# One block of 105 empty TensorE instructions, or 140 spread in fives: a cross-attention layer on one core

## The chip, the core and the metric

The kernel runs on one core of a Trainium2 chip. The metric is device time in microseconds (us), less is better. TensorE is called PE here (its weight loads PEld), VectorE DVE, ScalarE ACT, GpSimd POOL and SyncE SP. SP issues nearly all DMAs.

## The reference

128 sequences of 128 tokens, 256 features, 16 heads of 16 features, all in float32. `x` gives the queries, a second sequence `c` gives keys and values. What is computed, cut to its core:

```
q, k, v = heads(x @ Wq + bq), heads(c @ Wk + bk), heads(c @ Wv + bv)
scores  = q @ k.T / 4, and -1e30 wherever j >= i        # a strictly lower triangle
attn    = softmax(scores); the row i = 0 is set to 0
x1      = layer_norm(x + (attn @ v) @ Wo + bo, ln1)
out     = layer_norm(x1 + relu(x1 @ W1 + b1) @ W2 + b2, ln2)
```

The hidden layer has 1024 features.

## The kernel before

The batch is worked in 64 pairs of sequences. Each pair passes through several steps of a software pipeline, since its stages lie far apart: step p does the scores, the softmax and the values of pair p, the weighted sum and the output projection of pair p-2, the first hidden product of pair p-3, the second one of pair p-4, the second norm of pair p-6, and queries and keys of pair p+1.

Nothing is scheduled by a compiler. The order on every engine is the order in which the code is written. There are three stretches of it:

- **The front**: steps 0 to 8, written out; from step 7 on as a long list of `do("name", p)` calls, one operation a line. It ends with `do("h4", 7)` and `do("v4", 8)` (L2410 and L2411).
- **The steady part**: `for p in range(9, 61): step(p)`, 52 steps. `step` (L1761) walks the string `ORDER` (from L1746), in which every operation has its place; a suffix such as `-1` means that it belongs to the step before.
- **The tail**: steps 61 to 63, written out again.

What a step asks of PE, in the order of `ORDER`: `weigh` (L586 and L596: probabilities times values, 96 small matmuls in the trace, read from `brought`), `scores` (L440: 64 small matmuls, queries `qT` times keys `kT`), and then 30 products of five families. `v1` to `v4`, `o1` to `o4`, `q1` to `q4` and `k1` to `k4` (L1147, values, output, queries, keys) have 1 to 3 matmuls of 128x128 each, `w1` to `w7` (L1147, second hidden product) and `h1` to `h7` (L1358, first hidden product) 4 each. Each float32 matmul of the program appears as two MATMULs and two LDWEIGHTS in the trace.

Results of PE lie in eight banks of PSUM. `scores` writes all eight, so it needs what the other engines still read there to be done: the copies of the value product (`vr`, ACT L1272), `hf` (DVE L1383), and the rectified hidden layer (`re0` on DVE L1397, `re1` to `re3` on ACT L1399). `ro0` to `ro3` (ACT L1387) follow; they read no bank. `context` (DVE L612 and L617) takes the result of `weigh`. `h4` writes to a bank that `ha` (DVE L1377) has to have read.

SP's DMAs within a step, in order: `br0` to `br3` (L552: the transposed probabilities, `brought<-turned`, 128 KB each), the loads of a coming pair (L92: `xb` in one step, `cb` in the next, four of 128 KB each), in every second step a load of 512 KB of raw tokens (L99, `x<-in_x_dram`), the store of a finished pair (L765, 256 KB), and `ks2` and `ks` (L1235, `kT<-kr`, 128 KB each), which `scores` of the next step waits for.

`empty(n)` (L251) puts n instructions on PE that do nothing (NO_OP in the built program, NOP in the trace, L253). Two tables place them: `EMPTY` puts 2 to 5 behind each of the 30 products of a step of the steady part, 101 in all; `LEAD` puts n ahead of a whole step, and holds one entry, 105 ahead of step 9. The front's own products of steps 7 and 8 have none.

Counted in the built program, a step of the steady part has 768 PE instructions: 328 MATMULs, 328 LDWEIGHTS, 101 NOPs and 11 waits that stand by themselves. The whole PE program before has 48,035.

Of the kernel before, what the change touches and what calls it, by code (L numbers as in the profile page):

```python
# [19 lines left out]
def tile_cross_attention_block(  # L20
# [230 lines left out]
    def empty(n):  # L251
        for _ in range(n):
            nc.tensor.nop(hint="pad", nofuse=True)  # L253
# [1502 lines left out]
    """.split()  # L1756

    EMPTY = {'w1': 5, 'h1': 4, 'w2': 5, 'h2': 4, 'w3': 5, 'h3': 5, 'w4': 4, 'h4': 5, 'w5': 4, 'h5': 5, 'w6': 4, 'h6': 5, 'w7': 5, 'h7': 4, 'v1': 3, 'o1': 2, 'q1': 2, 'k1': 2, 'v2': 3, 'o2': 2, 'q2': 2, 'k2': 3, 'v3': 2, 'o3': 2, 'q3': 3, 'k3': 2, 'v4': 2, 'o4': 2, 'q4': 3, 'k4': 2}
    LEAD = {9: 105}

    def step(p):  # L1761

        empty(LEAD.get(p, 0))
        for key in ORDER:
            key, late = (key.split("-") + ["0"])[:2]
            q = p - int(late)
            if FIRST <= q < NP - 1:
                OPS[key](q)
                if key in EMPTY:
                    empty(EMPTY[key])  # L1770
# [76 lines left out]
    def do(key, p):  # L1847
        OPS[key](p)
# [443 lines left out]
    do("res1", 7)  # L2292
    do("eh6", 8)
    do("q1", 8)
    do("o1", 8)
    do("w1", 7)
    do("eh7", 8)
    do("w5", 7)
    do("add1", 8)
    do("lowmax", 8)  # L2300
    do("v3", 8)
    do("el0", 8)
    do("w2", 7)
    do("add2", 8)
    do("tokc", 7)
    do("qk", 8)
# [3 lines left out]
    do("xc1", 7)  # L2310
    do("max2", 8)
    do("o2", 8)
    do("wk", 7)
    do("finish1", 7)
    do("ok2", 8)
# [1 line left out]
    do("max1", 8)  # L2317
    do("el7", 8)
    do("k1", 8)
    do("xc3", 7)  # L2320
    do("cc1", 8)
    do("cc3", 8)
    do("add0", 8)
    do("vb", 8)
    do("w3", 7)
    do("q2", 8)
    do("max0", 8)
    do("el3", 8)
    do("o3", 8)
    do("tokx", 8)  # L2330
    do("w6", 7)
    do("load", 7)
    do("kk", 8)
    do("br3", 8)
# [4 lines left out]
    do("oa", 8)  # L2339
    do("xs0", 7)  # L2340
    do("k2", 8)
    do("qk2", 8)
    do("xs2", 7)
    do("o4", 8)
    do("q3", 8)
    do("xs1", 7)
    do("el5", 8)
    do("eh2", 8)
# [5 lines left out]
    do("res1", 8)  # L2354
    do("stats2", 8)
    do("w7", 7)
    do("or", 8)
    do("kk2", 8)
    do("h1", 7)
    do("va", 8)  # L2360
    do("qb", 8)
    do("eh4", 8)
# [3 lines left out]
    do("eh5", 8)  # L2366
    do("el4", 8)
    do("h2", 7)
    do("wb", 7)
    do("wa", 7)  # L2370
    do("stats1", 8)
    do("means", 8)
    do("el1", 8)
    do("k3", 8)
    do("w4", 7)
    do("deviations", 8)
    do("h6", 7)
    do("hk2", 7)
    do("qa", 8)
    do("hb", 7)  # L2380
# [2 lines left out]
    do("el2", 8)  # L2383
    do("kb", 8)
    do("h5", 7)
    do("hk5", 7)
    do("xc0", 8)
    do("ka", 8)
    do("wr", 7)
    do("k4", 8)  # L2390
    do("xc1", 8)
    do("store", 7)
    do("h7", 7)
    do("turn0", 8)
    do("turn1", 8)
    do("kr", 8)
    do("recip", 8)
    do("ks2", 8)
    do("q4", 8)
    do("ha", 7)  # L2400
    do("h3", 7)
    do("qr", 8)
    do("norm2", 8)
    do("turn2", 8)
# [3 lines left out]
    do("addbo", 8)  # L2408
    do("ks", 8)
    do("h4", 7)  # L2410
    do("v4", 8)  # L2411
    for p in range(9, 61):
        step(p)

# [650 lines left out]
```

## Time and profile before

| what | value |
|---|---|
| time, median of 3 runs (lowest, highest) | 1499.5 us (1498.47, 1502.43) |
| the profiled execution: its own time | 1498.78 us |
| the profiled execution: span, first to last instruction | 1497.0 us |
| mean granted TensorE clock over the span | 0.993 |
| DVE, ACT, POOL busy | 1374.0, 1304.2, 1265.4 us |
| one step in the middle, 239.66 to 261.68 us: PE, DVE, ACT, POOL busy | 21.85, 21.30, 20.88, 19.58 of 22.02 us |
| DMA: bytes moved, mean rate | 220.33 MB, 147 GB/s |

The times of the profile are counted from the span's start. "Busy" is the time in which an engine had an instruction in work. Sequencer work (NOPs, waits, DMA issues) does not count as busy. "Idle before" is the pause of an engine ahead of an instruction with what seems to have ended it; "issue" there means that nothing in the profile was waited for. Pauses below 0.15 us are not listed as such.

### The profile page before, as it was taken

Reading aid. Unit: us, or ns where it says so; the run is one execution under the profiler, and the core shown is the slowest. Engines: PE = TensorE matmul, PEld = TensorE weight load, DVE = VectorE, ACT = ScalarE, POOL = GpSimd, SP = SyncE. Lnnn points to the kernel's source line nnn. Section 1 sums busy time; section 2 is a strip of 40 time slices with the busy share of each in tenths; the row PEclk is TensorE's granted clock in tenths of the full one; section 3 lists DMA queues with packets and bytes.
Section 4 is the critical chain, followed back from the end, with each engine's and each line's share of the span. In section 5 each row is a group of like instructions: output and inputs, shape, how many; then the busy total and the mean of one; then the engine's idle time right before and its main releaser. Section 6 shows DMA issues by size and latency. Waiting matters only on the chain.

```text
span 1497.0 us, 61901 instructions
## 1 busy us (share of the span) xinstructions
PE 1458.7 (97%) x20713; PEld 1399.8 (94%) x20713; DVE 1374.0 (92%) x3231; ACT 1304.2 (87%) x5559; POOL 1265.4 (85%) x1816
## 2 busy tenths in 40 slices
PE   9999789999999999999999999999999999999998
PEld 7788789999999999999999999999999999999988
DVE  7987879999999999999999999999999999998767
ACT  5668879999989999999999999989999999998743
POOL 6967768888988988988988988988988988888966
PEclk9999999999999999999999999999999999999999
DMA  8274657666766766766766766766766766764541
GB/s 200 72 152 105 162 125 160 149 159 150 169 146 156 158 151 150 165 155 154 156 151 152 170 146 150 156 155 150 170 152 153 167 149 150 164 153 119 123 112 50
DMA packets 367448, 220.33 MB, mean 147 GB/s; under 512 B 279600, under 2 KB 335152, under 8 KB 367152
## 3 DMA queue, kind: packets, MB, share of 16 engines
q1 hardware_dynamic: 364864, 214.27, 63.1%
q8 instruction: 187, 3.06, 0.9%
q10 hardware_dynamic: 2288, 2.11, 0.6%
q14 instruction: 109, 0.89, 0.2%
HBM read 55.06 MB, written 18.09 MB: 49 GB/s over the span
## 4 chain that ended last, share of the span: by engine, by line
PE 75%; ACT 8%; DVE 6%; DMA 4%; SPq 3%; POOL 2%; issue 2%; DVEq 0%; ACTq 0%; POOLq 0%
PE banks L1147 38%; PE banks L1358 19%; ACT sm L931 6%; PE banks L440 5%; PE banks L596 3%; DMA kT<-kr 3%; SPq L552 2%; PE banks L869 2%; PE banks L586 2%; PE banks L300 1%; DMA brought<-turned 1%; PE banks L971 1%; PE banks L629 1%; DVE sm L464 1%; ACT kr L1213 1%
## 5 line engine op out<-in xcount | busy, mean ns | idle before, releaser
L931 ACT ACTIVATE sm<-banks,nmx 128x128 f32<-128x128 f32 x944 | 336.8, 383 | 16.4 <-DVE nmx L1558 12.8
L931 ACT ACTIVATE sm<-sm,nmx 128x64 f32<-128x64 f32 x944 | 321.6, 368 | 1.4 <-DVE nmx L920 1.4
L533 DVE STREAM_TRANSPOSE turned<-sm 128x1024 f32<-128x1024 f32 x186 | 217.1, 1214 | 4.7 <-DMA brought<-turned 2.9
L931 ACT ACTIVATION_READ_ACCUMULATOR sm<-banks,nmx 128x1 f32 x944 | 211.2, 224 | 0.0
L931 ACT ACTIVATION_READ_ACCUMULATOR sm<-sm,nmx 128x1 f32 x944 | 206.9, 219 | 0.0
L1147 PE MATMUL banks<-wt,hS 128*128 128x128 f32 x1344 | 177.5, 275 | 0.0
L1358 PE MATMUL banks<-xS,w1t 128*128 128x128 f32 x1344 | 177.2, 275 | 0.0
L1147 PEld LDWEIGHTS banks<-wt,hS 128*128 128x128 f32 x1344 | 163.6, 192 | 0.0
L1358 PEld LDWEIGHTS banks<-xS,w1t 128*128 128x128 f32 x1344 | 163.4, 192 | 0.0
L1558 DVE TENSOR_REDUCE nmx<-banks 128x4 f32<-128x512 f32 x224 | 152.3, 680 | 1.9
L1547 POOL TENSOR_TENSOR hS<-hT 128x512 f32<-128x512 f32 x116 | 147.7, 1274 | 5.0 <-ACT hT L876 2.4
L1358 PE MATMUL banks<-brought,w 128*128 128x128 f32 x896 | 118.2, 275 | 0.0
L1534 POOL TENSOR_TENSOR oc<-cxT 128x128 f32<-128x128 f32 x112 | 48.9, 457 | 80.4 <-DVE cxT L617 76.9
L1608 POOL TENSOR_TENSOR x1b<-x,g_r 128x512 f32<-128x512 f32 x56 | 72.3, 1290 | 52.3 <-ACT x L703 52.3
L1147 PE MATMUL banks<-w,hT 128*128 128x128 f32 x896 | 109.8, 275 | 0.0
L1358 PEld LDWEIGHTS banks<-brought,w 128*128 128x128 f32 x896 | 109.0, 192 | 0.0
L440 PE MATMUL banks<-kT,qT 32*64 32x128 f32 (+1 forms) x3840 | 101.2, 333 | 4.7 <-DMA kT<-kr 3.3
L1147 PEld LDWEIGHTS banks<-w,hT 128*128 128x128 f32 x896 | 104.8, 192 | 0.1
L440 PEld LDWEIGHTS banks<-kT,qT 32*64 32x64 f32 x3840 | 83.0, 132 | 15.5 <-issue 5.0
L1387 ACT ACTIVATE hT<-hT,b1e_c 128x256 f32<-128x256 f32 x224 | 95.7, 509 | 1.2 <-DVE hT L1383 1.1
L596 PE MATMUL banks<-brought,vz 128*32 128x64 f32 x4096 | 88.2, 223 | 6.6 <-issue 6.6
L1552 DVE TENSOR_TENSOR banks<-banks,neg 128x256 f32<-128x256 f32 x224 | 93.2, 417 | 0.0
(322 smaller groups left out, 4836.2 us busy)
## 6 DMA issues: line engine op xcount, KB each, us to landing
brought<-turned SPq DMA_DIRECT2D x936, 128.0 KB, 2.4
out_dram<-t SPq DMA_DIRECT2D x63, 256.0 KB, 4.6
xb<-in_x_dram SPq DMA_DIRECT2D x124, 128.0 KB, 3.1
cb<-in_ctx_dram SPq DMA_DIRECT2D x124, 128.0 KB, 3.2
x<-in_x_dram SPq DMA_DIRECT2D x31, 512.0 KB, 5.0
kT<-kr SPq DMA_DIRECT2D x112, 128.0 KB, 2.9
brought<-turned SPq DMA_DIRECT2D x40, 96.0 KB, 2.5
w<-in_L_xattn_W_dram SPq DMA_DIRECT2D x2, 1024.0 KB, 7.9
```

The costliest lines, as they stand in the source:

```text
L440: nc.tensor.matmul(st["sps", hi][r][s * HP : (s + 1) * HP, m * 2 * n : (m + 1) * 2 * n].rearrange("p (e j) -> p e j", e=2), st["qT"][strip ...
L533: nc.vector.transpose(turned[:, :, at : at + 256].rearrange("p j (n a) -> p n j a", a=32), states[p]["sm", hi].rearrange("p h j -> p (h j) ...
L596: nc.tensor.matmul(pc[32 * j : 32 * j + 32, at + HP : at + P], st["vz"][:, s, 4 * m + j, 2 * e : 2 * e + 2, :].rearrange("p e d -> p (e d) ...
L931: nc.scalar.activation(sm[:, h, :], src, AF.Exp, bias=nmx[:, h : h + 1], scale=1.0, **({"accum_out": st["su"][:, at : at + 1]} if summed e ...
L1147: nc.tensor.matmul(out, left(k) if self.depth > 1 else left, right(k) if self.depth > 1 else right, start=(n == 1 and k == 0), stop=(k == ...
L1358: nc.tensor.matmul(ps[:, i * P : (i + 1) * P].rearrange("p (n a) -> p n a", a=32), left(i), right, start=(n in (1, 2, 5) and i == 0), stop ...
L1387: nc.scalar.activation(self.hT[:, f, at], self.hT[:, f, at] if src is None else src, AF.Relu, bias=b1e_c[:, f : f + 1], scale=1.0,)
L1534: nc.gpsimd.tensor_tensor(c[:, n], left, right, how)
L1547: engine.tensor_tensor(c[:, n], left, right, how)
L1552: nc.vector.tensor_tensor(ps[:, :, HP:], ps[:, :, HP:], neg[:, 1, None, :].to_broadcast([P, 4, HP]), ALU.add)
L1558: nc.vector.tensor_reduce(states[p]["nmx", 1][:, 4 * b : 4 * b + 4], banks[:, b].rearrange("p (n j) -> p n j", j=P), AX.X, ALU.max, negate ...
L1608: nc.gpsimd.tensor_tensor(st["x1b"], st["x1b"] if n else st["x1"], (be1b_r if n else g1_r)[:, None, :].to_broadcast([P, 2, D]), ALU.add if ...
```

## The change

`LEAD` becomes empty, and 28 calls of `empty(5)` are put into the front, each behind one of the last 28 PE products that the front has for steps 7 and 8, from `q1` of step 8 to its last, `v4`. The diff, cut:

```diff
-    LEAD = {9: 105}
+    LEAD = {}
...
     do("q1", 8)
+    empty(5)
     do("o1", 8)
+    empty(5)
     do("w1", 7)
+    empty(5)
     do("eh7", 8)
     do("w5", 7)
+    empty(5)
...
     do("o4", 8)
+    empty(5)
     do("q3", 8)
+    empty(5)
...
     do("q4", 8)
+    empty(5)
     do("ha", 7)
     do("h3", 7)
+    empty(5)
...
     do("h4", 7)
+    empty(5)
     do("v4", 8)
+    empty(5)
     for p in range(9, 61):
         step(p)
```

Only PE's list of instructions changes; on DVE, ACT, POOL and SP the same operations stand in the same order. The built PE list at the end of the front (`q4`, `h3`, `h4` and `v4`, then the first matmuls of `weigh` of step 9), before:

```order
L1147 MATMUL banks<-xT_2247,wqt 128x128
L1358 MATMUL banks<-xS_2623,w_132 128x128 x4
L1358 MATMUL banks<-brought,w1t 128x128 x4
L1147 MATMUL banks<-wvt,cT_2245 128x128
L253 NO_OP x105
L586 MATMUL banks<-brought,vd_180 32x64 x8
```

The same place in the changed program:

```order
L1147 MATMUL banks<-xT_2247,wqt 128x128
L253 NO_OP x5
L1358 MATMUL banks<-xS_2683,w_132 128x128 x4
L253 NO_OP x5
L1358 MATMUL banks<-brought,w1t 128x128 x4
L253 NO_OP x5
L1147 MATMUL banks<-wvt,cT_2245 128x128
L253 NO_OP x5
L586 MATMUL banks<-brought,vd_180 32x64 x8
```

Five of the 105 are left between `v4` and `weigh`; the others are gone from this place. The middle of the front, where short products follow each other (`o3`, `w6`, `k2` and `o4`; `cc`, `oc` and `hS` are sums that POOL made), before and after as one difference:

```order
 L1147 MATMUL banks<-wot,oc_2443 128x128
+L253 NO_OP x5
 L1147 MATMUL banks<-wt,hS_2269 128x128 x4
-L1147 MATMUL banks<-cc_2563,wkt 128x128
-L1147 MATMUL banks<-cc_2563,wk 128x128
-L1147 MATMUL banks<-wot,cxT 128x128
+L253 NO_OP x5
+L1147 MATMUL banks<-cc_2593,wkt 128x128
+L1147 MATMUL banks<-cc_2593,wk 128x128
+L253 NO_OP x5
+L1147 MATMUL banks<-wot,cxT 128x128
+L253 NO_OP x5
```

Behind each product, five NOPs are new; the products themselves stand as they did (the numbers behind the names are buffers). All of the steady part and of the tail keeps its instructions, but stands 35 instructions further back in the PE program, which has 48,070.

More of the change, by code (lines that the diff above doesn't have):

```diff
@@ L2329, in tile_cross_attention_block @@
     do("o3", 8)
+    empty(5)
     do("tokx", 8)
     do("w6", 7)
+    empty(5)
     do("load", 7)
@@ L2341, in tile_cross_attention_block @@
     do("k2", 8)
+    empty(5)
     do("qk2", 8)
@@ L2344, in tile_cross_attention_block @@
     do("o4", 8)
+    empty(5)
     do("q3", 8)
+    empty(5)
     do("xs1", 7)
@@ L2356, in tile_cross_attention_block @@
     do("w7", 7)
+    empty(5)
     do("or", 8)
@@ L2359, in tile_cross_attention_block @@
     do("h1", 7)
+    empty(5)
     do("va", 8)
@@ L2368, in tile_cross_attention_block @@
     do("h2", 7)
+    empty(5)
     do("wb", 7)
@@ L2374, in tile_cross_attention_block @@
     do("k3", 8)
+    empty(5)
     do("w4", 7)
+    empty(5)
     do("deviations", 8)
     do("h6", 7)
+    empty(5)
     do("hk2", 7)
@@ L2385, in tile_cross_attention_block @@
     do("h5", 7)
+    empty(5)
     do("hk5", 7)
@@ L2390, in tile_cross_attention_block @@
     do("k4", 8)
+    empty(5)
     do("xc1", 8)
@@ L2393, in tile_cross_attention_block @@
     do("h7", 7)
+    empty(5)
     do("turn0", 8)
@@ L2399, in tile_cross_attention_block @@
     do("q4", 8)
+    empty(5)
     do("ha", 7)
     do("h3", 7)
+    empty(5)
     do("qr", 8)
@@ L2410, in tile_cross_attention_block @@
     do("h4", 7)
+    empty(5)
     do("v4", 8)
+    empty(5)
     for p in range(9, 61):
```

## The prediction

> **What bounds the kernel now.** I read the page first, then the waits of PE between 200 and 1400 us, then timelines.
>
> ```profile
> span 1497.0 us, 61901 instructions
> PE 1458.7 (97%) x20713; PEld 1399.8 (94%) x20713; DVE 1374.0 (92%) x3231; ACT 1304.2 (87%) x5559; POOL 1265.4 (85%) x1816
> q8 instruction: 187, 3.06, 0.9%
> PE banks L596 <- issue: 6.6, 14, 1.1
> PE banks L440 <- DMA kT<-kr: 3.3, 9, 0.7
> ```
>
> PE is busy 97% of the span. In the 1200 us of the steady part it waits (columns: us in total, times, longest) in two places only: 14 times inside `weigh` for "issue", which is nothing that the profile shows, and 9 times ahead of `scores` for the `kT` DMA. PE is the bound there, so a pause that leaves PE shortens the run by as much, unless another wait steps in. The timeline of PE where the front ends, and the windows beside it (busy us and count of PE, PEld, DVE, ACT, POOL; granted clock; DMA share and GB/s):
>
> ```profile
> 183.47 1.16 PE L1358 MATMUL banks<-brought,w1t 128*128 128x128 f32 x8 [0.90 <-DVE hT L1377]
> 184.46 0.39 PE L1147 MATMUL banks<-wvt,cT 128*128 128x128 f32 x2
> 191.87 0.66 PE L586 MATMUL banks<-brought,vd 128*32 128x64 f32 x16 [7.02 <-issue]
> 194.59 2.16 PE L440 MATMUL banks<-kT,qT 32*64 32x128 f32 x64
> ...
> 186.00:188.00 2.00, 0.00 (x0) 0.00 (x0) 0.73 (x2) 2.00 (x7) 0.06 (x1) 1.00 0.00 0
> 188.00:190.00 2.00, 0.00 (x0) 0.00 (x0) 0.00 (x0) 0.39 (x1) 0.00 (x0) 0.75 0.00 0
> 190.00:192.00 2.00, 0.13 (x8) 0.16 (x11) 0.00 (x0) 0.00 (x0) 0.00 (x0) 0.50 0.00 0
> 192.00:194.00 2.00, 2.00 (x81) 2.00 (x84) 0.00 (x0) 0.00 (x0) 0.00 (x0) 0.50 0.03 8
> 194.00:196.00 2.00, 2.00 (x67) 1.73 (x64) 0.89 (x4) 0.00 (x0) 0.39 (x1) 0.55 0.00 0
> ...
> L253 PEldq NOP  x93: 13/13/13, 184.5 to 191.4; - x93
> ```
>
> PE stands still for 7.02 us between `v4` (184.46) and `weigh` of step 9 (191.87). The last row, the NOPs between 184.5 and 192.5 us, says what it does: 93 of the 105 start there in 6.9 us, one every 75 ns (the 13 in the row is what the record calls their length). The other 12 ran while `h4` and `v4` were still at work. Behind the pause the granted clock is 0.50 until about 195 us, so `weigh` and `scores` run at half speed. From 189 to 194 us no engine does anything. This is one place where the whole chip waits for empty instructions.
>
> **The change, first part: the 105 go.** What `weigh` and `scores` cost at full clock is in any later step without a stall, such as step 11:
>
> ```profile
> 238.18 0.43 PE L586 MATMUL banks<-brought,vd 128*32 128x64 f32 x16
> 239.66 1.67 PE L440 MATMUL banks<-kT,qT 32*64 32x128 f32 x64
> ...
> 185.61 1.20 ACT L1399 ACTIVATE hT<-banks,b1e_c 128x256 f32<-128x256 f32 x3 [0.46 <-DVE hT L1397]
> 186.69 1.70 ACT L1387 ACTIVATE hT<-hT,b1e_c 128x256 f32<-128x256 f32 x4
> 197.66 0.27 ACT L1686 COPY vz<-banks 128x128 f32<-128x128 f32 x1 [9.26 <-PE banks L1147]
> 186.04 0.69 DVE L1614 STREAM_TRANSPOSE turned<-x 128x512 f32<-128x512 f32 x1
> 181.56 1.36 SPq L1235 DMA_DIRECT2D kT<-kr  x2
> kT<-kr SPq DMA_DIRECT2D x112, 128.0 KB, 2.9
> ```
>
> From the start of `weigh` to the end of `scores` step 11 takes 1.48 + 1.67 = 3.15 us; step 9 takes 191.87 to 196.75, 4.88. So the half clock costs 1.73 us.
>
> Without the block, `weigh` can start when `v4` is done, at 184.85, or 0.1 us later: `v4`'s own five NOPs (0.37 us) and four single waits come after it in the sequencer, which ran ahead of `v4`. Then `scores` starts at 184.95 + 1.48 = 186.4 and ends at 188.1. What it needs is there in time: `re1` to `re3` end at 186.81 and are needed in the second half of `scores`; `kT`'s two DMAs are issued by 182.92 and land 2.9 us after their issue, by 185.9; DVE is free for `context` from 186.73. Behind `scores`, ACT's first work for step 9 (197.66 before) moves to about 189.0, and `ro0` to `ro3` are done at 188.39. POOL and SP have nothing left from before. In step 10 the same ACT work ends about as long behind `weigh` as here, so nothing is compressed beyond what a normal step does.
>
> The term: 7.02 − 0.10 + 1.73 = **8.65 us less**. It is bounded above by 8.8 (no gap at all) and below by about 7: if `scores` had to wait for the end of ACT's `ro` (188.39) instead of starting at 186.4, 2.0 us would come back.
>
> **Second part: 140 NOPs behind the front's products.** At 75 ns five take 0.37 us of PE's sequencer. They cost nothing as long as the array still has queued work:
>
> ```profile
> 172.58 0.39 PE L1147 MATMUL banks<-wot,oc 128*128 128x128 f32 x2
> 172.80 1.06 PE L1147 MATMUL banks<-wt,hS 128*128 128x128 f32 x8
> 173.70 0.39 PE L1147 MATMUL banks<-cc,wkt 128*128 128x128 f32 x2
> ```
>
> A product of one program matmul occupies the array 0.22 us (172.58 to 172.80), one of four 0.90. Eight of the 28 have one matmul, so they fall short by 0.15 us each, 1.2 us in all if no lead is left; the long ones win 0.5 us each. The cover is the sequencer's lead. If it is gone everywhere, PE reaches `h4` up to 1.2 us late, and there it has 0.90 us to spare, since it waits for DVE until 183.47 anyway. I take 0 and bound it by 0 and 0.3 us.
>
> **Third part: everything behind stands 35 instructions later.** The q8 row counts 187 fetches of 3.06 MB, 16.4 KB each; the PE program has 48,035 instructions, so a fetch brings 257, or the round 256. A step has 768, three times that. So the borders between fetched blocks fall at the same three places in every step. One lies in `weigh`:
>
> ```profile
> 260.21 0.43 PE L586 MATMUL banks<-brought,vd 128*32 128x64 f32 x16
> 261.12 0.39 PE L596 MATMUL banks<-brought,vz 128*32 128x64 f32 x10
> 262.06 0.54 PE L596 MATMUL banks<-brought,vz 128*32 128x64 f32 x22 [0.55 <-issue]
> 262.52 0.69 PE L440 MATMUL banks<-kT,qT 32*64 32x128 f32 x24
> ...
> 217.17 0.54 PE L596 MATMUL banks<-brought,vz 128*32 128x64 f32 x22 [0.23 <-issue]
> 217.64 1.66 PE L440 MATMUL banks<-kT,qT 32*64 32x128 f32 x64
> 1378.20 1.10 PE L440 MATMUL banks<-kT,qT 32*64 32x128 f32 x29
> ...
> 239.66:261.68 22.02, 21.85 (x312) 21.34 (x306) 21.30 (x53) 20.88 (x93) 19.58 (x29) 1.00 0.74 169
> ```
>
> In steps 12 and 10, PE stops behind the tenth matmul of the last group, with 22 left: behind matmul 74 of 96, both times. All 14 stalls stand on L596. From `scores` of step 10 (217.64) to `scores` of step 62 (1378.20) are 52 steps in 1160.56 us; at 22.02 us for a step without a loss (the window in the last row, from `scores` of step 11 to the stall of step 12) they would take 1145.04. So **15.5 us** are lost at `weigh` and `scores`, more than the listed 6.6 + 3.3, since pauses below 0.15 us are not listed. All of it can be touched by a shift of the border.
>
> When is a block asked for? The place 256 instructions ahead of the stalling one has 26 NOPs between it and `weigh`; the place 35 further ahead has 31. Two answers on L253 (windows 209.6 and 209.0 to 215.6), two on DMA queues (214.8 to 216 and 231 to 234 us), and SP's timeline:
>
> ```profile
> L253 PEldq NOP  x26: 13/13/13, 209.6 to 214.5; - x26
> L253 PEldq NOP  x31: 13/13/13, 209.0 to 214.5; - x31
> q8 instruction: 1, 0.02, 4.9%
> q8 instruction: 1, 0.02, 3.3%
> 209.77 0.62 SPq L99 DMA_DIRECT2D x<-in_x_dram  x1
> ```
>
> In the products of step 9 the sequencer passes that place at about 209.5 us, and the fetch runs only between 214.8 and 216, some 5 us later (the stall at 217.17); in those of step 10, which has no 512 KB load, it runs before 234 and nothing stalls (238.18 above). In step 9 SP issues that load at 209.77, just behind the request. So the stall is a fetch that came out late from behind a big load, in every second step.
>
> In the changed kernel the border lies 35 instructions earlier in the step, still in `weigh`, behind matmul 56 or 57. PE gets there 17.5 x 15.4 ns = 0.27 us earlier (96 matmuls in 1.48 us), and the request goes out 0.6 us earlier by the NOPs. **Bounds**: if late fetches come out at the same time as before, because the load ahead of them sets it, each of 14 stalls grows by 0.27, 3.8 us more. If the 0.6 us pass through, each shrinks by 0.33, 4.6 us less. If the request gets ahead of the load in all steps, nearly the whole loss goes, 12 of 15.5 us, the rest staying with `kT`. The nearest row is the 0.6 us between request and load: 209.0 instead of 209.6, load at 209.77. I take **3 us less**, since part of each stall hides a wait for `kT` that takes its place.
>
> Runtime: NRT & Kernel Launch of the Trainium skill, section Instruction fetch mechanics, says that blocks of 256 instructions are fetched while the one before executes, and that crossing a border is mostly hidden. By it this term would be 0; the trace agrees with the size of the block (257 by count) and not with the hiding (6.6 us on L596).
>
> **The sum**: 8.65 + 0 + 3 = 11.7 us less. The profiled execution has a span of 1497.0 and took 1498.8 us, 1.8 around it; 1498.8 − 11.7 = 1487.1. The median of the runs is 0.7 above that execution: 1499.5 − 11.7 = **1488 us**. About 0.3%, 4.5 us, is what a measurement of this kernel tells from no change.
>
> **Rivals.**
>
> *The border in the new place costs nothing.* The request precedes the load in every second step, fetches come early, `kT`'s engine is not held up: 8.65 + 12 = 20.6 less, **1479 us**. For it: steps without the load never stall. Against: 0.6 us is a small head start, and the load's four smaller predecessors are already under way.
>
> *The new place is neutral or worse in the same steps.* Late fetches stay where they are, and stalls grow by 0.27 us: 8.65 − 3.8 = 4.9 less, **1494.6 us**; with the skill's hidden fetch or with gains and losses that cancel, 8.65 less, 1490.9.
>
> *Slower.* Also the steps without the load begin to stall at the border. Price: each of 52 steps 0.17 us makes up for the 8.65; with 0.55, the stall of step 12, in the 26 steps that have none, and 3.8 in the others, 14.3 + 3.8 − 8.65 = 9.5 more, **1509 us**. It decides from the point where the fetch of such a step starts later than about 2.4 us ahead of PE's arrival. Against: there the fetch ended before 234, over 4 us ahead of 238.18, and PE arrives only 0.27 us earlier.
>
> *The change doesn't hide the NOPs.* If every NOP of the 140 took its 75 ns from PE, 10.5 us would come back, 1498.5 us with the 3. Against: PE's lead and the 0.90 us in front of `h4`.
>
> **How the numbers follow.** Forecast (the lead gone, the border worth between −1 and +7 us): 0.50, 1483 to 1492, likeliest 1488. Border free: 0.20, 1478 to 1483. Border worse: 0.20, 1492 to 1496. Slower: 0.05. NOPs not hidden: 0.05. The range 1479 to 1496 leaves out the upper two and a little of the second. Faster by over 0.3% (below 1495.0): 0.50 + 0.20 + 0.15 = 0.85. Within: 0.05 of the border worse, 0.05 of the NOPs: 0.10. Slower: 0.05.
>
> **What would show it.** `weigh` of step 9 within 0.3 us behind the front's `v4`, clock 1.00 in all windows from 180 to 200 us, `scores` of step 9 near 186.4: first part. `h4` of the front still at 183.5, with a shorter wait on DVE L1377: second part. Stalls on L586 behind 56 or 57 matmuls instead of L596 behind 74, their sum against 6.6, and the 52 steps from `scores` to `scores` against 1160.6 us: third part. The prediction is wrong if those 52 steps take over 1165 or under 1152 us, or if the stretch before step 10 gains less than 7.

## The result and the profile after

The changed kernel takes 1478.36 us (median; 1476.86 to 1482.84) against 1498.99 us before: ratio **0.9864, 95% interval 0.9837 to 0.9891**. That is 20.6 us less where 11.7 were forecast, 0.6 us below the range. Beside later runs of the kernel before it gave 1480.4 (0.9876, 0.9855 to 0.9896) and 1482.0 us (0.9869, 0.9844 to 0.9893), so 18 to 20 us less. The profiled execution took 1482.84 us, the longest of the four. One profile, that of the 140 in a block below, fell into a disturbed state at a clock of 0.848, so that only the times of that kernel are used.

The head of the page, and PE's waits between 175 and 1400 us, after:

```profile
span 1481.1 us, 61936 instructions
PE 1454.3 (98%) x20713; PEld 1398.6 (94%) x20713; DVE 1372.5 (93%) x3231; ACT 1304.3 (88%) x5559; POOL 1266.1 (85%) x1816
...
PE banks L440 <- DMA kT<-kr: 3.0, 6, 0.9
PE banks L1358 <- DVE hT L1377: 3.0, 1, 3.0
PE banks L440 <- ACT vz L1272: 0.4, 1, 0.4
PE banks L440 <- ACT hT L1399: 0.2, 1, 0.2
```

The row "L596 <- issue: 6.6, 14" is gone, and so is the 7.02 us pause. One wait has grown: `h4` of the front now waits 3.0 us for DVE, 0.9 before. PE's timeline before, of `scores` and `v1` of step 8 and of `h3`; then after, of the same, of the end of the front and of `scores` of steps 9, 10, 12 and 62, and one window with its clock (the last number but two):

```profile
161.09 1.86 PE L440 MATMUL banks<-kT,qT 32*64 32x128 f32 x64
163.79 0.71 PE L1147 MATMUL banks<-wv,cT 128*128 128x128 f32 x4 [0.84 <-DVE sm L464]
...
181.51 1.06 PE L1358 MATMUL banks<-xS,w 128*128 128x128 f32 x8
```

```profile
162.26 2.05 PE L440 MATMUL banks<-kT,qT 32*64 32x128 f32 x64
164.86 0.71 PE L1147 MATMUL banks<-wv,cT 128*128 128x128 f32 x4 [0.55 <-DVE sm L464]
...
182.80 1.06 PE L1358 MATMUL banks<-xS,w 128*128 128x128 f32 x8
186.87 1.86 PE L1358 MATMUL banks<-brought,w1t 128*128 128x128 f32 x8 [3.00 <-DVE hT L1377]
188.51 0.63 PE L1147 MATMUL banks<-wvt,cT 128*128 128x128 f32 x2
189.08 0.66 PE L586 MATMUL banks<-brought,vd 128*32 128x64 f32 x16
191.24 1.67 PE L440 MATMUL banks<-kT,qT 32*64 32x128 f32 x64
213.27 1.67 PE L440 MATMUL banks<-kT,qT 32*64 32x128 f32 x64
258.25 1.59 PE L440 MATMUL banks<-kT,qT 32*64 32x128 f32 x64 [0.85 <-DMA kT<-kr]
1362.17 1.74 PE L440 MATMUL banks<-kT,qT 32*64 32x128 f32 x64
...
188.00:190.00 2.00, 2.00 (x42) 1.78 (x44) 1.79 (x4) 0.81 (x3) 0.00 (x0) 0.50 0.00 0
```

Where the 15.9 us between the two spans lie, from `scores` to `scores`:

| stretch | before | after | difference |
|---|---|---|---|
| start to step 8 (same program) | 161.09 | 162.26 | +1.2 |
| step 8 to step 9 | 33.50 | 28.98 | −4.5 |
| step 9 to step 10 | 23.05 | 22.03 | −1.0 |
| step 10 to step 62, 52 steps | 1160.56 | 1148.90 | −11.7 |
| step 62 to the end | 118.8 | 118.9 | +0.1 |

The steady part gave most of it, four times what I took; the front, up to `scores` of step 10, gave 5.5 us where I took 8.65. The first row is scatter: in the profiles used here `scores` of step 8 starts between 159.7 and 163.1 us, though the program up to there is the same.

### The profile page after: what moved, and what is told of

It is laid out like the page before. It is cut to its first block, busy times and chain, and to the rows that moved or that the text cites. A ratio compares the mean times of both kernels' runs of the same rounds, so it can differ in the third digit from the quotient of the medians.

```text
span 1481.1 us, 61936 instructions
## 1 busy us (share of the span) xinstructions
PE 1454.3 (98%) x20713; PEld 1398.6 (94%) x20713; DVE 1372.5 (93%) x3231; ACT 1304.3 (88%) x5559; POOL 1266.1 (85%) x1816
## 3 DMA queue, kind: packets, MB, share of 16 engines
q1 hardware_dynamic: 364864, 214.27, 63.6%
## 4 chain that ended last, share of the span: by engine, by line
PE 79%; ACT 7%; DVE 5%; POOL 3%; DMA 3%; SPq 2%; issue 1%; DVEq 0%; POOLq 0%; ACTq 0%
PE banks L1147 41%; PE banks L1358 20%; PE banks L440 6%; ACT sm L931 5%; PE banks L596 3%; PE banks L586 2%; PE banks L869 2%; DMA kT<-kr 2%; PE banks L300 1%; DVE sm L464 1%; PE banks L971 1%; SPq L552 1%; PE banks L629 1%; POOL sm L476 1%; POOL hS L1547 1%
## 5 line engine op out<-in xcount | busy, mean ns | idle before, releaser
L931 ACT ACTIVATE sm<-banks,nmx 128x128 f32<-128x128 f32 x944 | 336.3, 381 | 15.9 <-DVE nmx L1558 12.3
L1534 POOL TENSOR_TENSOR oc<-cxT 128x128 f32<-128x128 f32 x112 | 49.0, 457 | 63.6 <-DVE cxT L617 62.5
L703 ACT ACTIVATE x<-t,nb,sd 128x256 f32<-128x256 f32 x126 | 68.3, 591 | 21.0 <-POOL nb L726 13.6
```

The lines of the kernel that those rows point to most:

```text
L703: nc.scalar.activation(x1[:, s], t1[:, s], AF.Identity, bias=st["nb", 1][:, s], scale=sd[:, s])
L931: nc.scalar.activation(sm[:, h, :], src, AF.Exp, bias=nmx[:, h : h + 1], scale=1.0, **({"accum_out": st["su"][:, at : at + 1]} if summed e ...
L1534: nc.gpsimd.tensor_tensor(c[:, n], left, right, how)
```

## Experiments

In all tables "52 steps" is from `scores` of step 10 to `scores` of step 62 (1145.0 without a loss), and "late" counts the 26 even steps whose fetch for the border in or near `weigh` starts less than 1.75 us ahead of `weigh`, or after it. Both are read from the starts of `scores`, of `weigh` and of the packets of queue q8 in each trace.

**Pause and border apart.** First the pause without the border, 4 NOPs behind each of 21 products and 3 behind the last seven:

```diff
-    LEAD = {9: 105}
+    LEAD = {}
     do("q1", 8)
+    empty(4)
...
```

> The pause goes, the border stays: the same 28 places of the front get 105 NOPs in all (4 each, 3 in the last seven), LEAD is empty, so everything from step 9 on stands where it stood before. Theory (two separate terms, 8.65 us for the pause and about 12 for the border): only the first is gained, 1499.0 - 8.7 = 1490 us; 10 or more stalls on L596 behind matmul 74, fetches in even steps start 0.4 to 1.1 us before weigh, 52 steps from scores of step 10 to scores of step 62 near 1160. Rival (the pause itself had set the phase between SP's load and PE's fetch, and its removal alone ended the stalls): 1478 us, no stall on L596, 52 steps near 1149.

Then the border without the end of the pause:

```diff
-    LEAD = {9: 105}
+    LEAD = {9: 140}
```

> The border moves, the pause stays: LEAD is {9: 140}, nothing is put into the front. The pause grows by 35 x 75 ns = 2.6 us. Theory: 1499.0 - 11.7 + 2.6 = 1490 us; no stall on L586 or L596, even steps fetch 2.3 to 4.8 us before weigh, 52 steps near 1149. Rival (the pause set the phase, the border is innocent): 1499.0 + 2.6 = 1501.6 us, stalls remain.

The first took 1495.53 us against 1498.46 (0.9979, 0.9959 to 0.9998). Its stalls are there (18 steps late, 52 steps 1156.8):

```profile
PE banks L596 <- issue: 5.2, 11, 0.5
```

So the end of the pause alone does not end them; but it is worth 3 us by the medians, not 8.7. In its profile, the fastest of its ten runs, the front up to `scores` of step 10 is 5.3 us shorter (51.26 after `scores` of step 8 instead of 56.55); where the slower runs lost a part of that is not shown. The second took 1487.07 us (0.9921, 0.9897 to 0.9945): 11.4 less although the pause grew by 2.6 (35 times 75 ns; with the 70 more of the 175 below, `scores` of step 9 comes 5.2 us later in the profile), so the border is worth **14 us**. Without the pause it is worth 15.1 (1495.53 to 1480.40 for the changed kernel in the same runs). So the two terms add up within about 1 us, and both sizes of mine were wrong.

**Is it the 512 KB load?** The kernel before with one operation moved on SP:

```diff
-        load-1 loadx store-1 eh1 wb-1 ...
+        load-1 store-1 eh1 wb-1 ...
...
-        ... ha-1 qr h3-1 ks2 norm2
+        ... ha-1 qr h3-1 ks2 loadx norm2
```

> The kernel before with one operation moved: loadx (L99, the 512 KB load of every second step) goes from ahead of the store to behind ks2, SP's last DMA of the step, about 3 us later; PE's program and the border are as before. Theory (the load, issued just behind the request, is what holds the fetch up): the fetch of every step starts 2.5 to 5 us before weigh, no stall on L596, kT lands early in even steps too, 1499.0 - 12 to - 15 = 1484 to 1487 us. Rival 1 (fetches are late at this request time whatever SP does, for instance because of the four 128 KB loads or the store): stalls stay, 1497 to 1500. Rival 2 (the load only moves the trouble into the next step, to br and the fetch of the next border): stalls go, but waits for brought come, 1495 or more.

Measured: 1482.63 us, 0.989 (0.9871 to 0.991), 15.8 less with PE's program untouched; 52 steps 1145.94, no step late. SP's timeline of step 11's transfers, ahead of `weigh` of step 12 at 260.21 before and 259.65 here, before and then with the load moved:

```profile
255.05 0.60 SPq L99 DMA_DIRECT2D x<-in_x_dram  x1
255.77 0.44 SPq L765 DMA_DIRECT2D out_dram<-t  x1
257.25 1.39 SPq L1235 DMA_DIRECT2D kT<-kr  x2
```

```profile
253.80 0.63 SPq L765 DMA_DIRECT2D out_dram<-t  x1
256.70 1.37 SPq L1235 DMA_DIRECT2D kT<-kr  x2
258.12 0.59 SPq L99 DMA_DIRECT2D x<-in_x_dram  x1
```

The request goes out at the same place, 6.0 us ahead of `weigh`. With the load 0.9 us behind it, the fetch started 0.6 us ahead of `weigh`; with the load after `kT`, 3.1 us ahead. The load is what held the fetch up, and it held `kT` up too: PE waits for `kT` nowhere in these 52 steps.

**Is the longer wait in the front chance?** The changed kernel once more:

> The changed kernel once more, for a second profile. In its first profile h4 of the front waited 3.0 us for DVE (0.9 before) and weigh of step 9 ran at half clock. Theory (chance of one execution, a brought DMA that landed late): the wait is near 0.9 us again, clock 1.00 up to 200 us, weigh of step 9 near 185, span near 1476, median 1478. Rival (the NOPs in the front cause it): the wait of 3 us is there again.

`h4` waited 3.4 us (and 3.0 in the 105 spread). Not chance. DVE's timeline and the instruction queue between 176.5 and 182 us say why, after:

```profile
179.97 0.28 DVE L1293 TENSOR_TENSOR t<-banks,x1b 128x128 f32<-128x128 f32 x1
183.66 2.37 DVE L533 STREAM_TRANSPOSE turned<-sm 128x1024 f32<-128x1024 f32 x2 [3.41 <-DMA brought<-turned]
186.18 0.63 DVE L1377 TENSOR_TENSOR hT<-banks,hT 128x512 f32<-128x512 f32 x1
...
q8 instruction: 1, 0.02, 1.5%
```

and DVE before, where that window holds no q8 row:

```profile
180.26 2.37 DVE L533 STREAM_TRANSPOSE turned<-sm 128x1024 f32<-128x1024 f32 x2 [1.30 <-DMA brought<-turned]
```

DVE may overwrite `turned` only when the last `brought<-turned` DMA of step 8 has landed. Before, those transfers end at 179.72 and the next block of PE's code comes at 185.03. The NOPs in the front bring that request forward; the fetch runs from 180.93 to 182.24, and the last two packets of `brought` end only at 182.66 and 183.03. They stand behind the fetch: all others have ended by 181.65, the first of the two starts at 182.22, as the fetch ends, and the second when the first has ended. `ha` (L1377) follows the transpose, `h4` follows `ha`, and behind a pause of 3 us `weigh` runs at half clock once more (2.16 instead of 1.48 us).

**Other places for the border.** The changed kernel with the load late; 70 NOPs with the load late; 122 NOPs with the load where it was; no NOPs at all:

```diff
     do("q1", 8)
-    empty(5)
```

(all 28 times; `empty(3)` in the first 14 places and `empty(2)` in the others for 70, `empty(5)` in the first ten and `empty(4)` for 122)

> The changed kernel (140 NOPs spread) with loadx moved behind ks2 as well. In the profiles of the changed kernel and of the 105 spread, a code fetch runs from 178.6 to 182.2 us, in the tail of the front's brought DMAs; DVE's next transpose, which waits for the last of them, comes 2 to 3 us late and h4 of the front waits 3.0 to 3.4 us. Theory (the NOPs pull the front's border crossing from 183.6 to 178.0 us, so this fetch meets those DMAs in every execution): the wait of h4 is 2 us or more again, weigh of step 9 at half clock, no loss in the 52 steps (1146), 1498.5 - 15.8 - 8.65 + 4 = 1478 us. Rival (the wait is chance): h4 waits 0.4 to 0.9 us, 1474 us.

> 70 NOPs spread (three behind each of the first 14 of the 28 products, two behind the others), LEAD empty, loadx behind ks2. The front's crossing comes at about 180 us instead of 178.0, its fetch at about 181.5, after the last brought packet (179.7); the border in the steady part is 35 instructions later than in the kernel before, its request 4.0 us ahead of weigh instead of 6.0. Theory (collision in the front; no load behind the request): h4 waits 0.4 to 0.9 us, clock 1.00 at step 9, 52 steps near 1146, 1498.5 - 15.8 - 8.65 = 1474 us. Rival 1 (the wait of h4 belongs to any NOPs in the front): 3 us wait, 1478. Rival 2 (4.0 us ahead of weigh is too late even without the load): stalls in many steps at the border, 1485 or more.

> Half the shift: 122 NOPs spread, LEAD empty, loadx where it was. The border lies 17 instructions earlier than before instead of 35, the request goes out at 6.5 us ahead of weigh (6.0 before, 6.8 with 140), the load is issued 4.9 to 6.5 us ahead of weigh. Theory (what counts is how far the request is ahead of the load): part of the even steps fetch early, part late: loss in 52 steps between 4 and 12 us, 1480 to 1490. If a lead of 0.5 us is enough: 1149 for the 52 steps, as with 140, and 1480. If the place in weigh and not the request counts (L596 stalls, L586 does not): the border lies behind matmul 65, still on L596 or L586 by the half of the group, and 52 steps near 1157, 1490 or more.

> No NOPs in the front, LEAD empty, loadx where it was: the border moves 105 instructions later than before, behind about 30 of the 64 matmuls of scores, and the sequencer asks for it only 0.7 us ahead of weigh, some 3.0 us ahead of PE's arrival, in every step. Theory (a fetch needs 1.3 us at least from request to start and about 2.4 us from its start until PE can use it): every step stalls on L440 by 0.7 to 2.5 us, 52 steps near 1145 + 36 to 130, total 1515 to 1610 us, slower than before, although h4 waits 0.4 to 0.9 us and the pause is gone. Rival (the stall needs the big load; a late request in itself costs nothing): 1475 to 1482 us.

| kernel | median us | ratio (interval) | 52 steps | late | `h4` waits |
|---|---|---|---|---|---|
| 140, load late | 1477.5 | 0.9856 (0.9815 to 0.9896) | 1145.7 | 0 | 3.8 |
| 70, load late | 1489.55 | 0.9941 (0.9921 to 0.9961) | 1158.6 | 10 | 4.2 |
| 122 spread | 1492.91 | 0.9952 (0.9929 to 0.9975) | 1161.0 | 26 | 3.0 |
| none | 1539.99 | 1.0272 (1.0231 to 1.0314) | 1208.6 | 26 | 1.65 |

The first behaves as the collision theory says. The second falls to its second rival: with a request 4.0 us ahead of `weigh` 11 odd steps are late as well. Of these fetches 15 start only 0.4 to 0.5 us ahead of `weigh`, in eight even and seven odd steps; as many stalls are listed:

```profile
PE banks L596 <- issue: 8.2, 15, 0.8
```

Its `h4` waited 4.2 us, since the fetch started at 181.97 and `brought` ended at 183.68; I had placed it clear of them. In the third, half the shift ends no late fetch; I had expected a loss of 4 to 12 us in the 52 steps, and it is 16.0. The fourth is the slower case, by 40 us. Its PE timeline in step 11 and its waits (200 to 1400 us):

```profile
235.24 1.11 PE L440 MATMUL banks<-kT,qT 32*64 32x128 f32 x30
236.69 1.10 PE L440 MATMUL banks<-kT,qT 32*64 32x256 f32 x34 [0.34 <-issue]
...
PE banks L440 <- issue: 34.5, 52, 1.0
```

and `h4` of the front there, with a window behind it:

```profile
185.71 1.16 PE L1358 MATMUL banks<-brought,w1t 128*128 128x128 f32 x8 [1.65 <-DVE hT L1377]
...
188.00:190.00 2.00, 1.93 (x88) 1.31 (x84) 2.00 (x6) 2.00 (x6) 0.24 (x1) 1.00 0.00 0
```

Behind matmul 30 of `scores`, where the count put the border, PE stops in every step, load or not. From the fetch's start (234.44) to the matmul that goes on (236.69) are 2.25 us; in step 12 before it was 2.43 (259.63 to 262.06). From the request, 0.7 us ahead of `weigh`, to the fetch, in the middle 0.74 behind it, are 1.4 us; in the profile before the shortest is 1.0 (6.0 to 4.96 us ahead), so the 1.3 us that I took as the least is not one. In the front, where nothing is spread, the pause's end is worth what I had said: `scores` of step 9 comes 25.92 us behind that of step 8 instead of 33.50, 7.6 less, and the clock stays at 1.00.

**Both gains without the collision.** The load late, 35 NOPs at the end of the front and 35 more in each of steps 9 to 11:

```diff
-                    empty(EMPTY[key])
+                    empty(EMPTY[key] + (p < 12) * (1 + (key in MORE)))
...
     do("h3", 7)
-    empty(5)
+    empty(15)
```

> A version meant to keep every gain: loadx behind ks2; the 140 extra NOPs are split, 35 at the end of the front (5 behind q4, 15 behind h3, 12 behind h4, 3 behind v4, so that the front's crossing stays near 183 us), and 35 more in each of steps 9, 10 and 11 (one or two more behind each product). From step 12 on the border is where the changed kernel has it. Theory (h4's long wait comes from the code fetch in the tail of brought, not from NOPs as such): no fetch between 175 and 182 us, h4 waits 0.4 to 1.7 us, clock 1.00 at step 9, at most 1.5 us lost in steps 9 to 11, 1146 per 52 steps: 1473 us. Rival (any NOPs in the front make h4 wait): 3 us or more again, 1477.

> The changed kernel beside the run above on the same chip: 1478 to 1480 us, h4 of the front waits about 3 us with a code fetch between 176 and 182 us.

It took **1476.53 us**, 0.9831 (0.981 to 0.9853), where I had expected 1473; the changed kernel took 1481.97 in the same runs. It is not told apart from the 140 with the load late (0.9856, 0.9815 to 0.9896). The rows of `h4`, `weigh` and `scores` of step 9:

```profile
185.39 1.46 PE L1358 MATMUL banks<-brought,w1t 128*128 128x128 f32 x8 [2.30 <-DVE hT L1377]
...
187.21 0.66 PE L586 MATMUL banks<-brought,vd 128*32 128x64 f32 x16
...
189.76 1.68 PE L440 MATMUL banks<-kT,qT 32*64 32x128 f32 x64
```

No fetch runs between 176 and 182 us, and the wait falls to 2.3 us: between theory (1.7 at most) and rival (3). The half clock was not avoided: the granted clock is 0.53 from 186 to 188 us and 0.62 from 188 to 190, and `weigh` takes 2.55 us (187.21 to 189.76). Behind the 1.65 us of the kernel without NOPs it stayed at 1.00. Over the profiles here `h4` waits 0.4 to 2.7 us (middle value 2.0) where the fetch comes at 183.9 us or later (before, the load late, no NOPs, this one, and the blocks of 88, 122, 131, 158 and 175), and 3.0 to 4.2 (middle value 3.5) where it starts between 176 and 182 (the other eight, with NOPs spread). The fetch costs about 1.5 us there, and a part of the wait is scatter that was small in the profile of before: the same front waits 0.4 us with the load late and 2.0 to 2.7 with the longer and shorter blocks. That it is the fetch, and not the NOPs as such, the DMAs show. In five of the eight profiles the last `brought<-turned` lands 3.4 to 4.1 us after its issue, where it takes 2.3 to 2.4 in the profiles without a fetch that show its landing; in the other three the fetch comes before SP has issued them all, and one issue follows the one before it after 1.7 to 2.3 us instead of 0.64.

**How far must it move?** Blocks ahead of step 9, so that only the border differs:

```diff
-    LEAD = {9: 105}
+    LEAD = {9: 122}
```

(88, 131, 158 and 175 in the same way)

> LEAD {9: 88}: 17 later than before, request 5.1 us ahead of weigh, behind the load's issue in most even steps. Theory (a later request gives more late fetches): late in 20 or more of the even steps, 52 steps 1157 to 1163. Rival (the border lies later, so PE arrives later and stalls shrink): 1150 to 1157.

> LEAD {9: 122}, nothing in the front. The spread of 122 fetched late in all 26 even steps (stalls) although its request came 0.5 us earlier than in the kernel before. Theory (the place of the border decides, whatever the front does): again late in 20 or more of 26, fetches of odd steps near 3.0 us ahead of weigh, 52 steps 1158 to 1163. Rival (a lag that the front with NOPs handed on to SP and PE made it so): late in 10 to 18 as with 105 or fewer, 52 steps 1150 to 1157.

> LEAD {9: 131}: the border 26 instructions earlier than before, its request 6.7 us ahead of weigh. Theory (a sharp point between 122 and 140 beyond which the fetch is out ahead of the load): either like 140 (no late fetch, 52 steps 1148 to 1150) or like 122 (late in 20 or more, 1158 to 1163). Rival (a gradual gain with the head start): late in 5 to 15, 1152 to 1157.

> LEAD {9: 158}: 53 earlier than before. The border in weigh is clear of the load; the next border, which 175 brought to o1, is 17 instructions further on than with 175. Theory (a window between the two borders): no late fetch in weigh, losses behind scores below 0.15 us a step, 52 steps 1147 to 1151. Rival (the loss of 175 already begins): 1152 to 1157.

> LEAD is {9: 175}, nothing in the front, loadx where it was: a border 70 instructions earlier than before, its request 8.0 us ahead of weigh. The pause grows by 70 x 75 ns = 5.2 us. Theory (once the request is clear of the load, more head start brings nothing more): the gain of the 140 in a block, 14 us, stays: 1499 - 14 + 5.2 = 1490 us, 52 steps near 1148. Rival (each us of head start gains more, or the late state returns): 52 steps below 1146.5 or above 1155.

| NOPs in all | 52 steps | loss | late | request ahead of `weigh` |
|---|---|---|---|---|
| 0 | 1208.6 | 63.6 | 26 (and all odd) | 0.7 |
| 88 | 1166.2 | 21.1 | 24 | 5.1 |
| 105 (before; spread) | 1160.6; 1156.8 | 15.5; 11.8 | 19; 18 | 6.0 |
| 122 (block; spread) | 1161.3; 1161.0 | 16.2; 16.0 | 23; 26 | 6.5 |
| 131 | 1151.9 | 6.9 | 0 | 6.7 |
| 140 (three profiles) | 1148.9; 1147.5; 1147.8 | 3.9; 2.5; 2.7 | 0 | 6.8 |
| 158 | 1155.4 | 10.4 | 0 | 7.4 |
| 175 | 1155.9 | 10.8 | 0 | 8.0 |

The last column is an estimate from the starts of the NOPs ahead of `weigh`. For 88, 122 (block), 131 and 158 there is one run each, its profile: 1502.08, 1500.96, 1490.43 and 1495.00 us beside 1500.70 of the kernel before.

The point is sharp: 122 is late in nearly all even steps, wherever the NOPs stand, 131 in none. And it does not go on: 158 lost 10.4 us where I had expected at most 6, and 175 took 1499.36 us (0.999, 0.9975 to 1.0006) where I had expected 1490; its longer pause costs 5.2 of that. Waits of PE behind step 9 for 122, 131 and 158:

```profile
PE banks L596 <- issue: 9.0, 15, 1.2
```

```profile
PE banks L440 <- DMA kT<-kr: 5.9, 6, 1.7
```

```profile
PE banks L440 <- DMA kT<-kr: 8.4, 12, 1.2
```

Beyond the point the stall is gone, and the listed waits are for `kT`. With 175 they come to 3.3 us only, and the next border shows, at `o1` behind `scores` of step 11, which starts at 249.11 where 248.82 would follow without a pause (0.22 us behind 248.60, as 172.80 follows 172.58 before):

```profile
248.60 0.39 PE L1147 MATMUL banks<-wvt,cc 128*128 128x128 f32 x2
249.11 0.68 PE L1147 MATMUL banks<-wo,cxT 128*128 128x128 f32 x4
```

Its fetch started at 246.74, 2.37 us ahead of 249.11, close to the 2.25 and 2.43 of the stalls above. By the count that border is asked for when PE enters the block before it, in `weigh`; since it too moves earlier, more of the block is short matmuls, and less time is left between the two. How much of the 10.8 us this makes is not shown.

**What else holds a fetch up.** The 70 with store and load behind `ks2`:

```diff
-        load-1 loadx store-1 eh1 ...
+        load-1 eh1 ...
...
-        ... h3-1 ks2 norm2
+        ... h3-1 ks2 store-1 loadx norm2
```

> The kernel with 70 spread and the load late stalled in 15 steps, fetches 0.4 us ahead of weigh, 3.6 us behind the request, without the big load near. Here the store (L765, 256 KB, 4.9 to 6 us ahead of weigh) goes behind ks2 too. Theory (a fetch comes out behind whatever transfer SP has just issued, here the store): fetches 1.7 us or more ahead of weigh in all steps, no stall on L596, 52 steps near 1146 against 1158.6, total 1477 to 1479. Rival (the kT transfers, issued 3.0 and 2.2 us ahead of weigh, hold it up): stalls as before, 1490.

The stalls stay; PE's waits:

```profile
PE banks L596 <- issue: 11.5, 15, 1.2
```

The median is 1498.88 us (0.9983, 0.996 to 1.0006), and the 52 steps take 1162.9 us instead of 1158.6. I had expected 1477 to 1479, or 1490 with the rival; why the median lies 9 us above that is not shown. There are 15 stalls as before, but thirteen in odd steps and two in even ones, where it was seven and eight. So the place of the store changes which steps stall, and moving it does not end the stalls of a request 4.0 us ahead of `weigh`. The `kT` transfers, issued 3.0 and 2.2 us ahead of it, are the rival's cause; that they are it was not tried by itself.

## Why the prediction was wrong

What came lies nearest the rival at 1479 us. Pause, border and NOPs were the right places to look at; the sizes of the second and the third term failed, and both of the signs of being wrong came in the profile: the 52 steps took 1148.9 us, under 1152, and the stretch up to `scores` of step 10 gained 5.5, under 7. That the medians differ by the 20.6 us of that rival's sum is luck: its 8.65 was not reached, and the same two kernels differed by 18.1 and 17.9 us in the later runs.

**First part, 8.65 us: right for the removal.** Without any NOPs the stretch to `scores` of step 9 lost 7.6 us with `h4` waiting 0.75 us longer than before; with the 0.5 us of `scores` at full clock (2.16 to 1.67 in the changed kernel; they lie behind the start of `scores`) that is 8.85. One reading beside it was not right: the engines do not all stand still from 189 to 194 us; ACT works until 188.39, and PE is at work again from 191.87.

**Second part, "I take 0 and bound it by 0 and 0.3 us": wrong.** The cover by PE's lead held: from `v1` of step 8 to `h3` are 17.72 us before (163.79 to 181.51) and 17.94 after (164.86 to 182.80), 0.2 more. But I asked only what 140 NOPs cost on PE, not which code they make PE ask for, and when. A fetch was brought forward into the tail of `brought`, DVE came late, and the 0.90 us "to spare" became 3.0 us of waiting, with the half clock behind it: of 8.65 us the changed kernel shows 4.5, and 0.5 in its `scores`. The other 3.6 went as 2.2 ahead of `h4`, 0.7 in `h4` and `v4` and 0.7 in `weigh`, these at half clock. The row to read for it was there: DVE's transpose already waited 1.30 us for `brought` before.

**Third part, "I take 3 us less": mis-sized.** Profiles show 11.7 to 13.1 against the kernel before and 7.9 to 9.3 against the 105 spread, which has the same border; the block of 140 gives 14 by its time. I laid the 0.6 us of earlier request against the stall, as if a late fetch came 0.6 us sooner. Mostly a fetch here is not a little late: it starts either some 2 to 5 us ahead of `weigh` or close to it, and with the big load moved away and the request 6 us ahead always the former. I had the case ("if the request gets ahead of the load in all steps") and its price, 12 us, and gave it 0.20, because 0.6 us seemed a small head start. With the border moved the two ends came and not the middle: 23 and 26 late steps with 122, none from 131 on.

**"Late fetches stay where they are"** did not happen at 140, but it is what 122 did: the rival was right for half the shift. **Slower** (0.05) had the right mechanism and the wrong place: steps without the load do stall when the request leaves 3 us to PE's arrival, at the border in `scores`, 52 times. **The NOPs are not hidden** was wrong.

Runtime: NRT & Kernel Launch of the Trainium skill, section Instruction fetch mechanics, has the crossing mostly hidden; without NOPs it costs 34.5 us here in 52 stalls, with the load late and 140 nothing that the list of waits shows.

**What stays open**: why the point lies between 122 and 131. In the two profiles with 105, early and late fetches both occur with the load from 0.4 us ahead of the request to 0.9 us behind it, and with 122 they are late even with the load 1.3 us behind, so the order of request and load by itself doesn't decide. By the count the request was ahead of the load in 18 of the 19 late steps of the kernel before already, so the rival at 1479 had the outcome of the third part and not its whole reason. Nor was it tried why `kT` is waited for longer with 131 and 158 than with 140; the two have one profile each.

## What to carry to other kernels

Count the instructions of an unrolled loop and find where blocks of 256 end: here a border in a dense stretch of short matmuls stalled when the fetch met a large transfer, and either the border (by NOPs ahead of it) or the transfer (by another place in the queue) could be moved; the transfer was the surer of the two, since it left `kT` in time as well. When instructions are added for one border, look at every other border that moves with it, and at what is on the DMA queues there. Where an effect switches, forecast its two ends with their chances, not their middle.

## What was not expected of the hardware

One 16 KB code fetch of about 1.3 us delayed the end of 128 KB transfers beside it by some 2 us: the front's `brought` ended 18.1 to 19.4 us behind `scores` of step 8 in the nine profiles without it, 19.7 to 21.0 in the eight with it. Nine more NOPs, between 122 and 131, changed late fetches from 23 of 26 to none. And the time of a kernel with late fetches scatters more: the load late alone ran from 1482.4 to 1483.2 us, the 105 spread from 1489.7 to 1502.2.
